# Attention block with group norm: the output projection in plain fp32 column halves instead of split fp32r weights

## The chip, the core and the metric

The kernel runs on one core of a Trainium2 chip. The metric is device time in microseconds of one execution, input in HBM to output in HBM. Before the change it is 1597.04 us, the median of three runs (1596.77 to 1597.25).

## What is computed

```python
# x: (4, 512, 48, 48) fp32; t = 48 * 48 = 2304 tokens; 8 heads of d = 64; C = 512
hn  = group_norm(x)                         # 32 groups of 16 channels, with scale and bias
qkv = einsum('oc,bchw->bohw', qkv_w, hn) + qkv_b
q, k, v = fp16 parts of qkv.reshape(b, 3, 8, 64, t)
w   = softmax(einsum('bhct,bhcs->bhts', q * s, k * s))   # s = 64 ** -0.25 in fp16
a   = einsum('bhts,bhcs->bhct', w, v).astype(float32)
out = x + einsum('oc,bchw->bohw', proj_w, a) + proj_b
```

## The kernel before

**Tiling.** Channels lie on the 128 partitions, in NC = 4 chunks c. The 2304 tokens of a batch are cut into NQ = 5 blocks j, four of 512 columns and one of 256. Heads go in pairs: 4 pairs a batch, 16 pairs g in all, one head in partitions 0 to 63 and one in 64 to 127.

**The main stream.** The attention is a list of steps, `stream`, each of them three score tiles: six score matmuls (`scores`, L1066) and three exponentials on ScalarE (L1073), two steps later the weighted values into the bank `av` (`values`, L1091), and on VectorE the running sum of the exponentials (`add`, L1122). At a block's end a ones matmul gives the softmax sums (`sl`, L1150); VectorE copies them (`rows`, `slx`), two DMAs gather them in the tile `sums`, GpSimd tests whether they lie between two bounds (`check_sums`, L1188 and L1189), VectorE inverts them, DMAs spread the inverses over the partitions (`ib`), and GpSimd divides into the fp16 tile `att` (`divide`, L1215). The tests accumulate in `fine`; if one fails, a flag selects a general path at the very end.

**Side work.** Chains of matmuls for q and k (`pqk`, L802), v (`pv`, L854) and the output projection (`pr`, L948) stand in a list, `beside`. `fill(n)` issues from it at each step, after the weighted values and ahead of the next scores (in a step that closes a block, ahead of the weighted values), by nominal costs that are written in the code, 1.77 us for a projection chain of 512 columns. All side chains share one PSUM bank, `pw`. Nothing is reordered after that: each engine runs its instructions in the order of issue.

**The projection.** `att32` copies att in fp32 into tiles `a` (ScalarE or GpSimd, L942 and L940). The matmul form fp32r reads those as fp32 in reduced precision, so the weights are split ahead of time into a high part `whi` and a low part `wlo`, the remainder. For each row block m, `proj_chain` adds up four c, each with whi and wlo, 128 weight columns wide: 8 matmuls. VectorE adds the bias and the residual x that was loaded two chains earlier into one of RES = 4 tiles (`residual`, tag `res`; L975), and SyncE's queue stores the tile. Batch 0 is projected while batch 1 is attended, and so on. In the last batch blocks 2 to 4 are projected in two parts: three pairs c (FIRST) while the last pair is attended, the fourth (LAST) after it. The last nine steps stand in the tail, in the banks `ahead`, `rest`, `held` and `last_av`.

The qkv weights and the normalized x are plain fp32, and the q, k and v chains are written in two column halves, `lo` in (0, 64), each into its half of the bank's partitions.

The functions that the change touches, and what calls them:

Of the kernel before, what the change touches and what calls it, by code (L numbers as in the profile page):

```python
# [470 lines left out]
def fast_path(  # L471
# [11 lines left out]
):  # L483
    nc = tc.nc

    RES = NC
    const = ctx.enter_context(tc.tile_pool(name="const", bufs=1))
    xpool = ctx.enter_context(tc.tile_pool(name="xpool", bufs=1))
    qkp = ctx.enter_context(tc.tile_pool(name="qkp", bufs=3))
# [11 lines left out]
    hn = {}  # L501


    SPARE = {(1, 2): lambda c: ("res", RES), (1, 3): lambda c: (f"a32_{c}", 1)}

    def load_x(b, j, c, engine):

# [46 lines left out]
    nc.sync.dma_start(bv, brow.to_broadcast((P, C)))  # L554


    whi = const.tile([P, NC, C], F32R, name="whi")
    wlo = const.tile([P, NC, C], F32R, name="wlo")

    wproj = {}  # L560

    def load_wproj(c):
        wproj[c] = work.tile([P, C], F32, tag="res", bufs=RES, name=f"wproj_{c}")
        nc.sync.dma_start(wproj[c], proj_wT[bass.ts(c, P), :])

    def split_wproj(c):
        w = wproj.pop(c)
        nc.vector.tensor_copy(whi[:, c, :], w)
        nc.vector.tensor_tensor(
            wlo[:, c, :], w, whi[:, c, :].bitcast(F32), ALU.subtract  # L570
        )

    mhalf = const.tile([P, 2], F32, name="mhalf")
    nc.gpsimd.memset(mhalf, -0.5)
# [15 lines left out]
            channel_multiplier=sign,  # L590
        )

    fine = const.tile([P, 2 * QB // P], F32, name="fine")
    nc.gpsimd.memset(fine, 1.0)

# [310 lines left out]
    def in_two(b, j):  # L908

        return b == B - 1 and j >= NQ - 3  # L910
# [13 lines left out]
    def att32(b, j, pairs=range(NC), beside=None):  # L924
        o, n = QBLOCKS[j]
        for c in pairs:
            if left_over(b, j):
                t = xpool.tile([P, n], F32R, tag=f"x{c}_{j}", name=f"a32_{b}_{j}_{c}")
            elif in_two(b, j) and c in EARLY:
                t = xpool.tile(  # L930
                    [P, n], F32R, tag=f"x{2 * c + 1}_1", name=f"a32_{b}_{j}_{c}"
                )
            else:
                t = work.tile(
                    [P, QB], F32R, tag=f"a32_{c}", bufs=1, name=f"a32_{b}_{j}_{c}"
                )
            at32[b, j, c] = t[:, :n]
            source = atts[b * NPAIR + c][:, o : o + n]
            if beside or c in beside_exps() and not (pairs == LAST and left_over(b, j)):
                nc.gpsimd.tensor_copy(at32[b, j, c], source)  # L940
            else:
                nc.scalar.copy(at32[b, j, c], source)  # L942

    def proj_chain(b, j, m, ps, pairs=range(NC)):
        n = QBLOCKS[j][1]
        steps = [(c, w) for c in pairs for w in (whi, wlo)]
        for i, (c, w) in enumerate(steps):
            nc.tensor.matmul(  # L948
                ps[:, :n],
                w[:, c, bass.ts(m, P)],  # L950
                at32[b, j, c],
                start=(i == 0),
                stop=(i == len(steps) - 1),
            )

    FIRST, LAST = range(NC - 1), range(NC - 1, NC)

# [26 lines left out]
    def proj_piece(b, j, chunks, pairs=range(NC), ahead=None):  # L984
        def run():
            evacuate, store = proj_run(b, j, chunks, pairs)
            evacuate()
            if pairs == LAST:
                finished.add((j, chunks[0]))

            if pairs != FIRST:
                loads.append((now[0] + 1, store))
            if ahead is not None:
                loads.append((now[0] + 1, ahead))

        return piece(QB / 290.0 * len(pairs) / NC, run, True, True)

    def proj_pieces(b, j):

        def ahead(k):
            if k < len(proj_list) and not in_two(b, proj_list[k][0]):
                residual(b, *proj_list[k])

        def begin():
            if in_two(b, j):
                att32(b, j, LAST)
            elif (b, j) == (B - 1, 0):
                att32(b, j, range(len(EARLY), NC))  # L1010
            else:
                att32(b, j)
            if j == 0:
                ahead(0)
                ahead(1)

        pairs = LAST if in_two(b, j) else range(NC)
        chains = [
            proj_piece(b, j, chunks, pairs, lambda k=k: ahead(k + 2))
            for k, (jj, chunks) in enumerate(proj_list)  # L1020
            if jj == j
        ]
        return [piece(0.0, begin)], chains
# [138 lines left out]
    def rows(g, j, sl):  # L1162

        o, n = QBLOCKS[j]
        sx = work.tile([P, QB], F32, tag="rows", name=f"slx_{g}_{j}")
        nc.vector.tensor_copy(sx[:, :n], sl[:, :n])  # L1166
        sm = small.tile([P, 2, QB // P], F32, tag="sums", name=f"sums_{g}_{j}")
        for h in range(2):
            nc.sync.dma_start(sm[:, h, : n // P], sx[h * D : h * D + 1, :n])
        sums[g, j] = sm  # L1170
        return sx
# [7 lines left out]
        )  # L1179

    def check_sums(g, j):
        n = QBLOCKS[j][1]
        sm = sums[g, j][:, :, : n // P]
        ok = fine.rearrange("p (h i) -> p h i", h=2)[:, :, : n // P]
        for op, limit in ((ALU.is_ge, SUM_MIN), (ALU.is_le, SUM_MAX)):
            t = small.tile([P, 2, QB // P], F32, tag="in", name=f"in_{g}_{j}")
            t = t[:, :, : n // P]
            nc.gpsimd.tensor_scalar(t, sm, limit, None, op)  # L1188
            nc.gpsimd.tensor_tensor(ok, ok, t, ALU.mult)  # L1189

    def invert(g, j):
        n = QBLOCKS[j][1]
# [124 lines left out]
    for b in range(B):  # L1317
        g = b * NPAIR
        old = b - 1
        if b == 0:  # L1320
            for j in range(NQ):
                if j < NC:
                    put_run(load_wproj, j)
                if j > 0:
                    put_run(split_wproj, j - 1)
                put_qk(g + 1, 1, (j,))
                put_qk(g + 1, 0, (j,))
            for block in SPARE:
                put_run(reload, *block)
        put_qk(g + 2, 1)  # L1330
        put_qk(g + 2, 0)

        late = [j for j in range(NQ) if (b + 1, j) in SPARE]
        early = [j for j in range(NQ) if j not in late]
        tiles = {j: range(o // P, (o + n) // P, 2) for j, (o, n) in enumerate(QBLOCKS)}
        for j in early:
            put_v(b, 1, tiles[j])
        if b == B - 1:
            put_qk(g + 3, 1)
            put_qk(g + 3, 0, range(NQ - 1))  # L1340
            put_convert(old, 0)
            put_qk(g + 3, 0, (NQ - 1,))

            THIRD = range(len(EARLY), NC - 1)
            ahead = [
                (residual, b, j, chunks)
                for j in (NQ - 2, NQ - 3, NQ - 1)
                for jj, chunks in proj_list
                if jj == j
            ]  # L1350
            ahead += [
                (att32, b, j, (c,)) for j in (NQ - 2, NQ - 3, NQ - 1) for c in EARLY
            ]
            ahead.append((att32, b, NQ - 2, THIRD))
            for j in range(NQ):
                put_proj(old, j, ahead)
                if j + 1 < NQ:
                    put_convert(old, j + 1)
            assert not ahead

            ahead = [
                (att32, b, NQ - 3, THIRD),
                (att32, b, NQ - 1, THIRD),
                *((att32, b, 0, (c,), True) for c in EARLY),
            ]
            for j in (NQ - 2, NQ - 3, NQ - 1):
                put_first(b, j, ahead if j != NQ - 2 else [])
            put_convert(b, 0)
            put_proj(b, 0)
            put_convert(b, 1)  # L1370
            put_proj(b, 1)
            put_convert(b, NQ - 3)
            put_proj(b, NQ - 3)
            continue

        for j in early:
            if j == NQ - 1 and b > 0:
                put_convert(old, 0)
            put_qk(g + 3, 1, (j,))
            put_qk(g + 3, 0, (j,))  # L1380
            put_run(reload, b + 1, j)
        for j in late:
            put_v(b, 1, tiles[j])
            put_qk(g + 3, 1, (j,))
            put_qk(g + 3, 0, (j,))
        if b > 0:
            for j in range(NQ - 1):
                put_proj(old, j)
                put_convert(old, j + 1)
        put_v(b + 1, 0)  # L1390
        if b > 0:
            put_proj(old, NQ - 1)
        put_qk(g + 4, 1)
        put_qk(g + 4, 0)
        put_qk(g + 5, 1)
        put_qk(g + 5, 0)
# [116 lines left out]
    for n in range(end):  # L1513
# [20 lines left out]
        if n >= BEHIND and not inside:  # L1534
            values(stream[n - BEHIND])
        if block_at(n - BEHIND - 2):
            check_sums(*block_at(n - BEHIND - 2))
            invert(*block_at(n - BEHIND - 2))
        if block_at(n - BEHIND - 3):
            spread(*block_at(n - BEHIND - 3))  # L1540
# [2 lines left out]
            divide(*block_at(n - BEHIND - 4))  # L1543
        if not filled:
            fill(n)
        while joins:
            joins.popleft()()
        if n - BEHIND in soon:
# [153 lines left out]
```

## Time and profile before

| | |
|---|---|
| runs | 1596.77, 1597.04, 1597.25 us |
| profiled execution | span 1595.6 us, first to last instruction (1.4 us under the median; a time of its own is not listed beside the span) |
| TensorE clock granted | 0.999 of full |
| projection, L948 | 640 matmul records, 155.4 us busy |
| q and k, L802 | 2560 matmul records, 536.2 us busy |
| GpSimd's range test, L1188 and L1189 | 158 instructions each, 100.8 and 62.0 us |
| HBM | 60.7 MB read, 19.2 MB written, 50 GB/s over the span |

Each engine runs its own queue in order: PE (TensorE matmuls), PEld (its weight loads, beside the matmuls), DVE (VectorE), ACT (ScalarE), POOL (GpSimd), SP (SyncE, DMA issue). A row of groups reads: line, engine, operation, out<-in, shapes, count, then busy us and mean ns of one, then the idle time ahead of them and what ended it. In rows of PE, 128*64 is weight rows times weight columns. A busy time counts modelled ends of matmuls, which reach into the next; the distance from start to start is free of that. In a timeline row like instructions are merged (x16), and its first number is the start of the first.

### The profile page before, as it was taken

To read this page: it belongs to the slowest core of one execution; us is meant where nothing else is said; L and a number is where in the kernel's file an instruction comes from. 1 tells how busy PE (TensorE), PEld (TensorE's weight loads), DVE (VectorE), ACT (ScalarE), POOL (GpSimd) and SP (SyncE) were. 2 spreads that over 40 slices of the span, in tenths; PEclk is the share of its full clock that TensorE was granted. 3 is DMA by queue.
4 is the path that set the end of the run, shared out by engine and by line. 5 is a ranking of instruction groups with operands and counts; after the bars stand their busy time and mean duration, and the time that the engine had idled before them with its cause. 6 is when DMAs were issued, how large, how long until landed. Compare 5 with 4: busy or idle time off the path is not lost. (4 is left out here: it accounts for less than half of the span.)

```text
span 1595.6 us, 28731 instructions
## 1 busy us (share of the span) xinstructions
PE 1582.0 (99%) x11526; PEld 701.7 (44%) x11526; DVE 1140.2 (71%) x1302; ACT 1269.4 (80%) x1363; POOL 336.8 (21%) x463
## 2 busy tenths in 40 slices
PE   9999999999999999999999999999999999999997
PEld 3733434443333534545333354455533334434554
DVE  6267668876666678887666666888767676767776
ACT  4177777888888888888888888887878888888885
POOL 1001202222121222312112121222212121121232
PEclk9999999999999999999999999999999999999999
DMA  7002020000000024521000001353101000015424
GB/s 222 3 14 67 12 73 16 18 14 12 15 18 11 12 69 119 144 67 28 11 14 18 14 12 41 111 158 88 23 17 18 15 15 11 15 31 166 149 62 133
DMA packets 94896, 82.10 MB, mean 51 GB/s; under 512 B 50852, under 2 KB 60964, under 8 KB 94756
## 3 DMA queue, kind: packets, MB, share of 16 engines
q1 hardware_dynamic: 92724, 78.35, 18.1%
q8 instruction: 92, 1.51, 0.4%
q10 hardware_dynamic: 1904, 1.84, 0.4%
q14 instruction: 48, 0.39, 0.1%
q0 software_dynamic: 128, 0.01, 0.0%
HBM read 60.70 MB, written 19.17 MB: 50 GB/s over the span
## 5 line engine op out<-in xcount | busy, mean ns | idle before, releaser
L1073 ACT ACTIVATE p<-ps 128x1024 f16<-128x1024 f32 x1296 | 1233.5, 1025 | 299.1 <-PE ps L1066 296.3
L1122 DVE TENSOR_TENSOR acc<-acc,p 128x3072 f16<-128x3072 f16 x270 | 485.4, 1798 | 53.8 <-ACT p L1073 51.3
L802 PE MATMUL pqk<-x,wqkv 128*64 128x512 f32 (+1 forms) x2432 | 510.3, 549 | 0.1
L1091 PE MATMUL av<-p,v 128*64 128x512 f16 (+1 forms) x2880 | 360.6, 364 | 0.0
L1066 PE MATMUL ps<-q,k 64*128 64x512 f16 (+1 forms) x2880 | 355.8, 358 | 0.4 <-DVE v L862 0.2
L854 PE MATMUL pv<-wqkv,x 128*64 128x256 f32 x2304 | 267.6, 379 | 0.3 <-DVE v L862 0.3
L802 PEld LDWEIGHTS pqk<-x,wqkv 128*64 128x64 f32 x2432 | 168.5, 137 | 205.4 <-issue 155.9
L1188 POOL TENSOR_SCALAR in<-sums 128x8 f32<-128x8 f32 (+1 forms) x158 | 100.8, 638 | 712.4 <-DMA sums<-slx 705.8
L1066 PEld LDWEIGHTS <-k 64*128 64x128 f16 x2880 | 105.9, 94 | 287.2 <-issue 238.2
L1091 PEld LDWEIGHTS <-v 128*64 128x64 f16 x2880 | 131.2, 109 | 212.8 <-issue 168.1
L1215 POOL TENSOR_TENSOR att<-avx,ib 128x512 f16<-128x512 f32 (+1 forms) x78 | 133.1, 1706 | 422.9 <-DMA ib<-row 373.7
L854 PEld LDWEIGHTS pv<-wqkv,x 128*64 128x64 f32 x2304 | 166.3, 137 | 81.3 <-DVE v L862 0.8
L1122 DVE TENSOR_TENSOR acc<-p,p 128x3072 f16<-128x3072 f16 x79 | 138.1, 1748 | 0.0
L948 PE MATMUL pr<-a,whi 128*128 128x512 f32 (+1 forms) x311 | 121.8, 399 | 0.1
L1127 DVE TENSOR_TENSOR acc<-acc 128x1024 f16<-128x1024 f16 x156 | 114.7, 735 | 3.3
L948 PE MATMUL pr<-a,wlo 128*128 128x512 f32 (+1 forms) x311 | 113.5, 372 | 0.0
L813 DVE TENSOR_SCALAR q<-pqk,bqkv 128x512 f16<-128x512 f32 (+1 forms) x77 | 53.5, 694 | 76.0 <-PE pqk L802 75.5
L813 DVE TENSOR_SCALAR k<-pqk,bqkv 128x512 f16<-128x512 f32 (+1 forms) x75 | 52.2, 695 | 77.7 <-PE pqk L802 77.5
L862 DVE TENSOR_TENSOR v<-pv,bv 128x512 f16<-128x512 f32 x72 | 49.7, 690 | 79.6 <-PE pv L854 79.5
L1166 DVE COPY slx<-sl 128x512 f32<-128x512 f32 (+1 forms) x79 | 50.6, 641 | 64.1 <-PE sl L1150 64.1
L975 DVE SCALAR_TENSOR_TENSOR r<-pr,bproj,r 128x512 f32<-128x512 f32 (+1 forms) x80 | 54.9, 695 | 41.3 <-PE pr L948 36.6
L1100 DVE COPY avx<-av 128x512 f32<-128x512 f32 (+1 forms) x79 | 50.6, 640 | 36.4 <-PE av L1091 36.1
(124 smaller groups left out, 506.7 us busy)
## 6 DMA issues: line engine op xcount, KB each, us to landing
r<-x_dram SPq DMA_DIRECT2D x72, 256.0 KB, 3.6
out_dram<-r SPq DMA_DIRECT2D x69, 256.0 KB, 2.4
ib<-row SPq DMA_DIRECT2D x126, 128.0 KB, 3.1
x<-x_dram SPq DMA_DIRECT2D x62, 256.0 KB, 3.9
x<-x_dram SPq DMA_DIRECT2D x16, 128.0 KB, 4.8
sums<-slx SPq DMA_DIRECT2D x128, 2.0 KB, 2.1
ib<-row SPq DMA_DIRECT2D x30, 64.0 KB, 3.0
wqkv<-qkv_wT_dram SPq DMA_DIRECT2D x2, 768.0 KB, 6.9
```

The costliest lines, as they stand in the source:

```text
L802: nc.tensor.matmul(pw[0][lo : lo + D, :n], wqkv[:, c, w0 + lo : w0 + lo + D], hn[b, c, j], start=(c == 0), stop=(c == NC - 1),)
L813: nc.vector.tensor_scalar(qk[g][part][:, o : o + n], pw[0][:, :n], bqkv[:, col : col + 1], SCALE, ALU.add, ALU.mult,)
L854: nc.tensor.matmul(pw[0][lo : lo + D, a, :], hn[b, c, i * P // QB][:, at + lo : at + lo + D], wqkv[:, c, 2 * C + half * C // 2 :][:, : C / ...
L948: nc.tensor.matmul(ps[:, :n], w[:, c, bass.ts(m, P)], at32[b, j, c], start=(i == 0), stop=(i == len(steps) - 1),)
L975: nc.vector.scalar_tensor_tensor(xt[:, i], places[i], bias, xt[:, i], ALU.add, ALU.add)
L1066: nc.tensor.matmul(ps[:, h, a * n : (a + 1) * n], kt[rows, bass.ts(i, P)], qt[rows, o : o + n], start=True, stop=True,)
L1073: nc.scalar.activation(pt[:, r], ps, AF.Exp)
L1091: nc.tensor.matmul(av[0][lo : lo + D, :n], vv[b, pr // 2][:, i, pr % 2 * P + lo : pr % 2 * P + lo + D], pt[:, r, h, a * n : (a + 1) * n], ...
L1122: nc.vector.tensor_tensor(t, before, pt, ALU.add)
L1127: nc.vector.tensor_tensor(t[:, 0], t[:, 0], t[:, r], ALU.add)
L1188: nc.gpsimd.tensor_scalar(t, sm, limit, None, op)
L1215: nc.gpsimd.tensor_tensor(atts[g][:, o : o + n], avx.pop((g, j))[:, :n], ibs.pop((g, j))[:, :n], ALU.mult,)
```

## The change

The projection's weights stay in plain fp32 in one tile `wproj`; `whi`, `wlo` and the eight VectorE instructions of the split are gone. `proj_chain` takes, for each c, the two column halves lo = 0 and 64 in place of whi and wlo, with `a` in fp32. There are six residual tiles instead of four, and residuals are loaded four chains ahead instead of two; the tiles `a` for chunks 2 and 3 get a second copy. The sums go into two standing tiles `sums_0` and `sums_1` that pairs use in turn, and `check_sums` tests a pair's 40 columns at once after its last block (for the last pair in two parts), issued behind the division and the filler instead of ahead of them.

```diff
-    RES = NC
+    RES = NC + 2
+    LEAD = RES - 2
+    def copies(c):
+        return 1 if c < NC // 2 else 2
...
-    whi = const.tile([P, NC, C], F32R, name="whi")
-    wlo = const.tile([P, NC, C], F32R, name="wlo")
+    wproj = const.tile([P, NC, C], F32, name="wproj")
...
-        nc.sync.dma_start(wproj[c], proj_wT[bass.ts(c, P), :])
-
-    def split_wproj(c):
-        w = wproj.pop(c)
-        nc.vector.tensor_copy(whi[:, c, :], w)
-        nc.vector.tensor_tensor(
-            wlo[:, c, :], w, whi[:, c, :].bitcast(F32), ALU.subtract
-        )
+        nc.sync.dma_start(wproj[:, c, :], proj_wT[bass.ts(c, P), :])
...
+    for s in range(2):
+        t = const.tile([P, NQ, 2, QB // P], F32, name=f"sums_{s}")
+        nc.gpsimd.memset(t, SUM_MIN)
+        sums_of.append(t)
...
                 t = work.tile(
-                    [P, QB], F32R, tag=f"a32_{c}", bufs=1, name=f"a32_{b}_{j}_{c}"
+                    [P, QB], F32, tag=f"a32_{c}", bufs=copies(c), name=f"a32_{b}_{j}_{c}"
                 )
...
     def proj_chain(b, j, m, ps, pairs=range(NC)):
         n = QBLOCKS[j][1]
-        steps = [(c, w) for c in pairs for w in (whi, wlo)]
-        for i, (c, w) in enumerate(steps):
-            nc.tensor.matmul(
-                ps[:, :n],
-                w[:, c, bass.ts(m, P)],
-                at32[b, j, c],
-                start=(i == 0),
-                stop=(i == len(steps) - 1),
-            )
+        for c in pairs:
+            for lo in (0, D):
+                nc.tensor.matmul(
+                    ps[lo : lo + D, :n],
+                    wproj[:, c, m * P + lo : m * P + lo + D],
+                    at32[b, j, c],
+                    start=(c == pairs[0]),
+                    stop=(c == pairs[-1]),
+                )
...
             if j == 0:
-                ahead(0)
-                ahead(1)
+                for k in range(LEAD):
+                    ahead(k)
...
-            proj_piece(b, j, chunks, pairs, lambda k=k: ahead(k + 2))
+            proj_piece(b, j, chunks, pairs, lambda k=k: ahead(k + LEAD))
...
-        sm = small.tile([P, 2, QB // P], F32, tag="sums", name=f"sums_{g}_{j}")
+        sm = sums_of[g % 2][:, j]
...
+        ends = (NQ - 1,) if g < NG - 1 else (NQ - 3, NQ - 2)
+        if j not in ends:
+            return
+        first = NQ - 2 if g == NG - 1 and j == NQ - 2 else 0
+        cols = slice(first * PER, (j + 1) * PER)
...
         if block_at(n - BEHIND - 2):
-            check_sums(*block_at(n - BEHIND - 2))
             invert(*block_at(n - BEHIND - 2))
...
         if not filled:
             fill(n)
+        if block_at(n - BEHIND - 2):
+            check_sums(*block_at(n - BEHIND - 2))
```

On PE, the first projection chain of batch 0, with the score weight load that follows it. Before (`pr` is the bank, `a` the copies of att):

```order
L948 MATMUL pr_0_0_6427<-a_0_0_0_6292,whi 128x512
L948 MATMUL pr_0_0_6427<-a_0_0_0_6292,wlo 128x512
L948 MATMUL pr_0_0_6427<-a_0_0_1_6294,whi 128x512
L948 MATMUL pr_0_0_6427<-a_0_0_1_6294,wlo 128x512
L948 MATMUL pr_0_0_6427<-a_0_0_2_6296,whi 128x512
L948 MATMUL pr_0_0_6427<-a_0_0_2_6296,wlo 128x512
L948 MATMUL pr_0_0_6427<-a_0_0_3_6298,whi 128x512
L948 MATMUL pr_0_0_6427<-a_0_0_3_6298,wlo 128x512
L1066 LDWEIGHTS k_4172
```

The same place on PE after the change, with the last matmul ahead of it; x2 stands for two rows that read alike, the two column halves:

```order
L1093 MATMUL av_3_6181<-p_3_2_6140,v_1_2956 64x512
L948 MATMUL pr_0_0_6256<-a_0_0_0_6124,wproj 64x512 x2
L948 MATMUL pr_0_0_6256<-a_0_0_1_6126,wproj 64x512 x2
L948 MATMUL pr_0_0_6256<-a_0_0_2_6128,wproj 64x512 x2
L948 MATMUL pr_0_0_6256<-a_0_0_3_6130,wproj 64x512 x2
L1068 LDWEIGHTS k_4069
```

The chain keeps its place and its eight matmuls; each now covers 64 output rows instead of 128. Elsewhere on PE almost nothing moves.

On PE at the end of the program, the last six steps, before:

```order
L948 MATMUL rest_16551<-a_3_3_3_16473,whi 128x512
L948 MATMUL rest_16551<-a_3_3_3_16473,wlo 128x512
L948 MATMUL rest_16551<-a_3_3_3_16473,whi 128x512
L948 MATMUL rest_16551<-a_3_3_3_16473,wlo 128x512
L948 MATMUL held<-a_3_4_3_16560,whi 128x256
L948 MATMUL held<-a_3_4_3_16560,wlo 128x256
L948 MATMUL held<-a_3_4_3_16560,whi 128x256
L948 MATMUL held<-a_3_4_3_16560,wlo 128x256
L948 MATMUL last_av<-a_3_4_3_16560,whi 128x256
L948 MATMUL last_av<-a_3_4_3_16560,wlo 128x256
L948 MATMUL last_av<-a_3_4_3_16560,whi 128x256
L948 MATMUL last_av<-a_3_4_3_16560,wlo 128x256
```

And after, from `ahead` to the matmul that counts the tests:

```order
L948 MATMUL ahead_16075<-a_3_2_3_15869,wproj 64x512 x2
L948 MATMUL rest_16086<-a_3_3_3_16013,wproj 64x512 x4
L948 MATMUL rest_16091<-a_3_3_3_16013,wproj 64x512 x4
L948 MATMUL held<-a_3_4_3_16100,wproj 64x256 x4
L948 MATMUL last_av<-a_3_4_3_16100,wproj 64x256 x4
L1646 MATMUL count<-ones,good 1x1
```

The number of matmuls and their order are the same here too.

On GpSimd, the first blocks of pair 0, before (`in` and `fine` are the range test, `att` the division, NO_OP a placeholder):

```order
L1188 TENSOR_SCALAR in_0_1019<-sums_0_975 128x8
L1189 TENSOR_TENSOR fine<-fine,in_0_1019 128x8
L1188 TENSOR_SCALAR in_0_1022<-sums_0_975 128x8
L1189 TENSOR_TENSOR fine<-fine,in_0_1022 128x8
L780 NO_OP x2
L1215 TENSOR_TENSOR att_748<-avx_0_943,ib_0_1065 128x512
```

And after, from block 3 of the same pair on:

```order
L1220 TENSOR_TENSOR att_750<-avx_3_1652,ib_3_1781 128x512
L780 NO_OP
L1193 TENSOR_SCALAR in_4_1883<-sums_167 128x40
L1194 TENSOR_TENSOR fine<-fine,in_4_1883 128x40
L1193 TENSOR_SCALAR in_4_1886<-sums_167 128x40
L1194 TENSOR_TENSOR fine<-fine,in_4_1886 128x40
L780 NO_OP x2
L1220 TENSOR_TENSOR att_750<-avx_4_1779,ib_4_1911 128x256
```

The divisions of blocks 0 to 3 have no test ahead of them any more, and one test of 40 columns stands where the last block's was.

More of the change, by code (lines that the diff above doesn't have):

```diff
@@ L501, in fast_path @@
     hn = {}
-    SPARE = {(1, 2): lambda c: ("res", RES), (1, 3): lambda c: (f"a32_{c}", 1)}
+    SPARE = {(1, 2): lambda c: ("res", RES), (1, 3): lambda c: (f"a32_{c}", copies(c))}
     def load_x(b, j, c, engine):
@@ L554, in fast_path @@
     nc.sync.dma_start(bv, brow.to_broadcast((P, C)))
-    whi = const.tile([P, NC, C], F32R, name="whi")
-    wlo = const.tile([P, NC, C], F32R, name="wlo")
-    wproj = {}
+    wproj = const.tile([P, NC, C], F32, name="wproj")
     def load_wproj(c):
-        wproj[c] = work.tile([P, C], F32, tag="res", bufs=RES, name=f"wproj_{c}")
-        nc.sync.dma_start(wproj[c], proj_wT[bass.ts(c, P), :])
-    def split_wproj(c):
-        w = wproj.pop(c)
-        nc.vector.tensor_copy(whi[:, c, :], w)
-        nc.vector.tensor_tensor(
-            wlo[:, c, :], w, whi[:, c, :].bitcast(F32), ALU.subtract
-        )
+        nc.sync.dma_start(wproj[:, c, :], proj_wT[bass.ts(c, P), :])
     mhalf = const.tile([P, 2], F32, name="mhalf")
@@ L591, in fast_path @@
         )
-    fine = const.tile([P, 2 * QB // P], F32, name="fine")
+    PER = 2 * QB // P
+    fine = const.tile([P, NQ * PER], F32, name="fine")
     nc.gpsimd.memset(fine, 1.0)
+    sums_of = []
+    for s in range(2):
+        t = const.tile([P, NQ, 2, QB // P], F32, name=f"sums_{s}")
+        nc.gpsimd.memset(t, SUM_MIN)
+        sums_of.append(t)
     alone = [True]
@@ L927, in att32 @@
             if left_over(b, j):
-                t = xpool.tile([P, n], F32R, tag=f"x{c}_{j}", name=f"a32_{b}_{j}_{c}")
+                t = xpool.tile([P, n], F32, tag=f"x{c}_{j}", name=f"a32_{b}_{j}_{c}")
             elif in_two(b, j) and c in EARLY:
                 t = xpool.tile(
-                    [P, n], F32R, tag=f"x{2 * c + 1}_1", name=f"a32_{b}_{j}_{c}"
+                    [P, n], F32, tag=f"x{2 * c + 1}_1", name=f"a32_{b}_{j}_{c}"
                 )
@@ L1002, in ahead @@
         def ahead(k):
-            if k < len(proj_list) and not in_two(b, proj_list[k][0]):
+            if k >= len(proj_list) or in_two(b, proj_list[k][0]):
+                return
+            if (b, proj_list[k][0], proj_list[k][1][0]) not in res:
                 residual(b, *proj_list[k])
@@ L1181, in check_sums @@
     def check_sums(g, j):
-        n = QBLOCKS[j][1]
-        sm = sums[g, j][:, :, : n // P]
-        ok = fine.rearrange("p (h i) -> p h i", h=2)[:, :, : n // P]
+        ends = (NQ - 1,) if g < NG - 1 else (NQ - 3, NQ - 2)
+        if j not in ends:
+            return
+        first = NQ - 2 if g == NG - 1 and j == NQ - 2 else 0
+        cols = slice(first * PER, (j + 1) * PER)
+        sm = sums_of[g % 2].rearrange("p j h i -> p (j h i)")[:, cols]
         for op, limit in ((ALU.is_ge, SUM_MIN), (ALU.is_le, SUM_MAX)):
-            t = small.tile([P, 2, QB // P], F32, tag="in", name=f"in_{g}_{j}")
-            t = t[:, :, : n // P]
+            t = small.tile([P, NQ * PER], F32, tag="in", name=f"in_{g}_{j}")[:, cols]
             nc.gpsimd.tensor_scalar(t, sm, limit, None, op)
-            nc.gpsimd.tensor_tensor(ok, ok, t, ALU.mult)
+            nc.gpsimd.tensor_tensor(fine[:, cols], fine[:, cols], t, ALU.mult)
     def invert(g, j):
@@ L1323, in fast_path @@
                     put_run(load_wproj, j)
-                if j > 0:
-                    put_run(split_wproj, j - 1)
                 put_qk(g + 1, 1, (j,))
@@ L1364, in fast_path @@
                 *((att32, b, 0, (c,), True) for c in EARLY),
+                *((residual, b, *proj_list[k]) for k in range(2)),
             ]
```

## The prediction

> **What bounds the kernel now.** I read the page's busy shares first, then the stretches in which projections run, then single chains on TensorE's timeline.
>
> ```profile
> PE 1582.0 (99%) x11526; PEld 701.7 (44%) x11526; DVE 1140.2 (71%) x1302; ACT 1269.4 (80%) x1363; POOL 336.8 (21%) x463
> L1073 ACT ACTIVATE p<-ps 128x1024 f16<-128x1024 f32 x1296 | 1233.5, 1025 | 299.1 <-PE ps L1066 296.3
> ```
>
> A busy PE alone proves little, since ends of matmuls are modelled. The second row says it from the other side: ScalarE, next in load, stands idle 299.1 us ahead of its exponentials, and 296.3 us of that ends with a score matmul. The exponentials wait for PE, not PE for them. The stretches (start:end, length, then busy time and records by engine) show whether that holds where projections run; the second row has none.
>
> ```profile
> 629.00:749.00 120.00, 120.00 (x931) 66.70 (x930) 100.52 (x131) 99.53 (x110) 30.69 (x39) 1.00 0.32 90
> 749.00:1036.00 287.00, 287.00 (x2089) 112.24 (x2089) 200.81 (x208) 239.29 (x253) 58.83 (x82) 1.00 0.13 32
> 1440.00:1577.00 137.00, 136.85 (x868) 73.36 (x866) 101.27 (x109) 119.65 (x136) 39.43 (x53) 1.00 0.45 131
> ```
>
> In both projection stretches PE has no idle time worth naming (0 and 0.15 us), at a granted clock of 1.00; VectorE has 19.5 and 35.7 us left, ScalarE 20.5 and 17.3. So what a projection chain takes on PE, from its first matmul to the first matmul of the next work, is paid in full, and the case reduces to that price before and after.
>
> **The chain before.** A full chain is four steps c, each with whi and wlo, 128 weight columns wide. Timeline of PE, columns start and duration in us:
>
> ```profile
> 639.79 0.50 PE L948 MATMUL pr<-a,whi 128*128 128x512 f32 x1
> 640.13 0.39 PE L948 MATMUL pr<-a,wlo 128*128 128x512 f32 x1
> 640.36 0.40 PE L948 MATMUL pr<-a,whi 128*128 128x512 f32 x1
> ...
> 641.53 0.40 PE L948 MATMUL pr<-a,wlo 128*128 128x512 f32 x1
> 641.86 0.83 PE L1066 MATMUL ps<-q,k 64*128 64x256 f16 x12
> ```
>
> Inside the chain a record follows the last at 0.23 us (640.13 to 640.36): a split weight costs one record each for whi and wlo. The chain holds PE for 641.86 - 639.79 = 2.07 us.
>
> **The chain after.** Plain fp32 weights in two halves of 64 columns against an fp32 moving tile of 512: this form is in the trace already, as the q/k chains (L802) and, 256 wide, as the v chains (L854).
>
> ```profile
> L802 PE MATMUL pqk<-x,wqkv 128*64 128x512 f32 x1936 | 451.7, 592 | 0.1
> 373.40 3.60 PE L802 MATMUL pqk<-x,wqkv 128*64 128x512 f32 x16
> 376.83 0.81 PE L1091 MATMUL av<-p,v 128*64 128x512 f16 x6
> 808.24 3.60 PE L802 MATMUL pqk<-x,wqkv 128*64 128x512 f32 x16
> 811.77 0.82 PE L1066 MATMUL ps<-q,k 64*128 64x512 f16 x6
> 339.21 3.62 PE L854 MATMUL pv<-wqkv,x 128*64 128x256 f32 x32
> 342.77 0.82 PE L1066 MATMUL ps<-q,k 64*128 64x512 f16 x6
> ```
>
> A whole q/k chain is written as 4 steps of 2 halves, 8 matmuls; the trace has 16 records, two per matmul. It holds PE for 3.43 us where the weighted values follow and 3.53 us where scores follow: 0.86 us a step, plus 0.10 us for the turn to the 64-row score matmuls. Halves run beside each other, but each needs twice the records and each pair of records takes 0.43 us. So the new chain stands in the program with as many matmuls as the old one and holds PE 1.36 to 1.46 us longer.
>
> **The sum.** How many chains there are follows from the loops (4 batches x 4 row blocks m x 4 steps c, for four blocks j of 512 columns and one of 256: 256 and 64 steps), and the records by shape bear it out: 251 and 60 of whi below, and 5 and 4 under the tail's names.
>
> ```profile
> L948 PE MATMUL pr<-a,whi 128*128 128x512 f32 x251 | 106.4, 424 | 0.1
> L948 PE MATMUL pr<-a,whi 128*128 128x256 f32 x60 | 15.4, 295 | 0.0
> 1503.86 0.39 PE L948 MATMUL pr<-a,whi 128*128 128x256 f32 x1
> ...
> 1505.96 0.82 PE L1066 MATMUL ps<-q,k 64*128 64x512 f16 x6
> 1516.89 0.50 PE L948 MATMUL pr<-a,whi 128*128 128x512 f32 x1
> ...
> 1518.48 0.84 PE L1091 MATMUL av<-p,v 128*64 128x512 f16 x6
> 1577.61 0.50 PE L948 MATMUL pr<-a,whi 128*128 128x512 f32 x1
> ...
> 1578.27 1.50 PE L1091 MATMUL av<-p,v 128*64 128x256 f16 x24
> ```
>
> - Full chains of 512: 16 in each of three batches and 8 in the last, 56. If all stand before scores 56 x (3.53 - 2.07) = 81.8 us, if none does 56 x (3.43 - 2.07) = 76.2. A filler is issued after the weighted values and ahead of the next scores, except in steps that close a block, so I take 81.
> - Pieces of two 256 chains, 2 in each of three batches: from 2.10 us (1503.86 to 1505.96) to the v row's 3.56: 6 x 1.46 = 8.8.
> - Last batch, three steps c (FIRST), 8 of 512 columns: from 1.59 us (1516.89 to 1518.48) to 3 x 0.86 + 0.10 = 2.68: 8.7. The 2 pieces of 256, at six of eight steps of the same rows: 2 x (2.67 - 1.58) = 2.2.
> - Single steps (LAST) issued beside the last blocks: 3, from 0.66 us (1577.61 to 1578.27) to 0.86 to 0.96: 0.9.
>
> That is 101.6 us up to the tail. The tail has nine more steps, and there PE isn't alone on the path:
>
> ```profile
> 1582.33 0.50 PE L948 MATMUL ahead<-a,whi 128*128 128x512 f32 x1
> 1583.10 0.59 ACT L1592 COPY beyond_ahead<-ahead 128x512 f32<-128x512 f32 x1
> 1583.15 0.50 PE L948 MATMUL rest<-a,whi 128*128 128x512 f32 x1
> 1584.12 1.29 POOL L1595 TENSOR_TENSOR r<-beyond_ahead,r 128x512 f32<-128x512 f32 x1 [0.46 <-ACT beyond_ahead L1592]
> 1586.08 0.28 PE L948 MATMUL last_av<-a,wlo 128*128 128x256 f32 x1
> 1588.13 0.43 DVE L1640 TENSOR_REDUCE good<-fines 128x1 f32<-128x264 f32 x1 [0.49 <-POOL fines L1627]
> 1588.48 0.68 DVE L971 TENSOR_TENSOR r<-last_av,r 128x512 f32<-128x512 f32 x1
> ```
>
> Now the last output's addition starts at 1588.48, 2.1 us after PE is through with it, because VectorE does `good` first, which waits for GpSimd. After: `ahead` ends at 1582.33 + 0.86 = 1583.19, four `rest` steps at 1586.6, four steps of 256 columns at 0.43 at 1588.3 and their data some 0.25 later. The copy of `ahead` moves 0.4 later and GpSimd's row of work behind it too, so `good` starts near 1588.5 and the addition near 1588.9. PE's 2.2 us are nearly covered; +0.4 remains.
>
> 101.6 + 0.4 = 102.0 us on the profiled execution's span of 1595.6, which lies 1.4 below the median of the runs, 1597.04. Forecast: 1699 us, 6.4% slower.
>
> **The parts that cost nothing.** Covers and bounds, by rows:
>
> ```profile
> L1188 POOL TENSOR_SCALAR in<-sums 128x8 f32<-128x8 f32 (+1 forms) x158 | 100.8, 638 | 712.4 <-DMA sums<-slx 705.8
> L568 DVE CAST whi<-wproj 128x512 fp32r<-128x512 f32 x4 | 1.7, 417 | 0.0
> L569 DVE TENSOR_TENSOR wlo<-wproj,whi 128x512 fp32r<-128x512 f32 x4 | 2.8, 693 | 0.1
> PEld pr L948 <- DVE r L975: 4.9, 15, 0.6
> ```
>
> The split goes: 4.5 us of VectorE in batch 0, where PE runs the q/k chains of L802, idle 0.1 us in all ahead of them. The range test goes from 158 pairs of GpSimd instructions to 34 on up to 40 columns and moves behind the division; GpSimd is busy 21% and was waiting for the sums' DMAs anyway, so the division starts a little sooner, which no chain needs. The sums' DMAs now write one of two standing tiles in turn, last read one pair's length earlier, about 1596 / 16 = 100 us, so no queue stalls on it. The four weight loads and 72 residual loads are the same in number; residual loads go two chains earlier on SyncE's queue into two more tiles, well ahead of their use. Copies of att write fp32 in place of fp32r; the trace shows none of that kind, and I take the old duration, with ScalarE's 17 us and more of slack in each stretch as cover. What could be gained from more tiles is bounded by waits around the chains: weight loads waited 4.9 us for the addition that frees the bank, but beside a PE that was still streaming. I take 0, with -5 as the far end.
>
> **Rivals.**
> - *Half the records.* If a plain fp32 half needed one record instead of two, a step would take 0.43 us and a full chain 4 x 0.43 + 0.10 = 1.82, shorter than 2.07: 56 x -0.25, with the shorter ones in proportion another -4, gives -18, 1579 us. It decides from a step below 0.49 us. For it speaks that both programs have eight matmuls per chain; against it 16 records in each whole q/k chain. The Trainium skill, "Perfetto Trace Analysis", section "Engine Utilization", has TensorE's output rate merely halved for FP32_LOW_HIGH, which is this rival; "FP8 and Floating Point Precision", section "TensorE Precision Notes", has true fp32 as four passes. By the first the step is 0.43 us, by the second 0.85, both as estimates; the measured 0.86 sides with the second. Chance 0.02.
> - *PE isn't the limit there.* If exponentials set the pace in the projection stretches, a chain's extra time would vanish in PE's waits: 1597. Against it stand the full PE and ScalarE's 20 us of idle time in 120. Chance 0.01.
> - *Waits go too.* The added tiles and lighter VectorE and GpSimd take the 4.9 us out after all: 1694. Chance 0.05.
> - *A longer end.* The tail pays PE's full 2.2 us, or as much again where 640 more matmul records shift what each engine has fetched by then, which no row prices; 4 us in all, an estimate: 1703. Chance 0.05.
>
> **How the numbers follow.** The main case has 0.87. Its terms vary between the two follower prices (-5 us if all stand before weighted values, +1 if all before scores) and the tail's 0 to +2. Low end 1692, where the waits go too and part of the follower term; high end 1705, a longer end with all chains at the dearer price and a microsecond of spread. A change of 0.2%, 3.2 us, is what can be told from none. Faster 0.02 (half the records), same 0.01 (PE not the limit), slower 0.97.
>
> **What would show it.** Right: L948 has twice the matmul records, 64 columns wide; a full chain takes 3.4 to 3.5 us; the three projection stretches grow by about 26, 26 and 49 us (16 x 1.45 + 2 x 1.46 for one batch, the rest of the sum for the last), PE still full and ScalarE idle longer; the rest of the program keeps its length. Wrong: chains near 1.8 us, or PE with idle time beside projections, or another stretch that changes by more than 3 us.

## The result

The changed kernel takes 1691.78 us, median of five runs (1691.31 to 1692.12), beside 1597.04 before: 94.7 us more, ratio 1.0594 (95% interval 1.0581 to 1.0607). The forecast was 1699, range 1692 to 1705. It is too high by 7.2 us, and the measured time lies just below the range.

The page after: busy shares, the chain that ended last (by engine), ScalarE's exponentials, the projection.

```profile
PE 1678.5 (99%) x12166; PEld 686.5 (41%) x12166; DVE 1136.1 (67%) x1294; ACT 1270.3 (75%) x1363; POOL 218.6 (13%) x217
PE 98%; DVE 1%; DMA 0%; ACT 0%; issue 0%; POOL 0%; DVEq 0%
L1075 ACT ACTIVATE p<-ps 128x1024 f16<-128x1024 f32 x1296 | 1233.3, 1025 | 391.8 <-PE ps L1068 390.4
L948 PE MATMUL pr<-a,wproj 128*64 128x512 f32 (+1 forms) x1244 | 254.1, 552 | 0.0
```

640 more matmul records, all of the projection. The exponentials take as long as before (1233.3 beside 1233.5) and wait 94.1 us more for PE (390.4 beside 296.3): PE's added time reaches the end one for one. GpSimd's busy time fell by 118.2 us (218.6 beside 336.8) and VectorE's by 4.1, and neither shows in the time. The stretches with projections (start:end, length, busy by engine) still have a full PE:

```profile
629.00:773.00 144.00, 144.00 (x1088) 62.41 (x1086) 99.89 (x131) 99.73 (x110) 17.56 (x19) 1.00 0.25 74
1060.00:1205.00 145.00, 144.84 (x1056) 60.80 (x1052) 101.21 (x128) 100.34 (x111) 21.81 (x19) 1.00 0.26 73
1490.00:1671.00 181.00, 181.00 (x1166) 66.03 (x1166) 99.63 (x109) 118.89 (x135) 32.46 (x33) 1.00 0.32 96
```

From the first projection record of one batch to that of the next (629.0, 1035.6 and 1445.5 us before, 628.9, 1060.0 and 1494.2 after) the program grew by 24.5 and 24.4 us, and from the last of these to the end by 45.6; ahead of the first it kept its length. The forecast had 26, 26 and 49. Each of the three stretches came out shorter than forecast, so the missing 7 us are not in one place; spread over some 75 chains they are about a tenth of a microsecond each.

**Where they are.** Here is one chain after, in PE's timeline, with the work ahead of it and behind it, and then, of the kernel before, weighted values ahead of a projection chain and ahead of a q/k chain:

```profile
658.31 0.85 PE L1093 MATMUL av<-p,v 128*64 128x256 f16 x12
658.99 3.60 PE L948 MATMUL pr<-a,wproj 128*64 128x512 f32 x16
662.52 0.82 PE L1068 MATMUL ps<-q,k 64*128 64x512 f16 x6
```

```profile
639.02 0.84 PE L1091 MATMUL av<-p,v 128*64 128x512 f16 x6
639.79 0.50 PE L948 MATMUL pr<-a,whi 128*128 128x512 f32 x1
...
407.70 0.84 PE L1091 MATMUL av<-p,v 128*64 128x512 f16 x6
408.38 1.88 PE L802 MATMUL pqk<-x,wqkv 128*64 128x512 f32 x8
```

The chain after holds PE for 662.52 - 658.99 = 3.53 us, the forecast price. But look at the weighted values *ahead* of a chain, before: six matmuls hold PE for 0.77 us where a projection follows (639.02 to 639.79) and for 0.68 where a q/k chain follows. From the last of them to the next matmul pass 0.31 us in the one case and 0.21 in the other (medians over 56 and 180 places). The projection's old chain was 128 weight columns wide and its neighbours are 64: the turn into it cost 0.10 us, and that time stands in front of the chain's first record, under another line. It isn't the weight load's wait for the bank: at 42 of the 56 places the profile shows no engine or transfer that the chain's first weight load waited for, and the gap there is 0.309 or 0.310 us; where VectorE's addition was waited for, it is 0.309 or 0.310 in five of seven, 0.329 and 0.526 in the others. After the change the weighted values ahead of a projection end at 0.21 us like all others. Over the whole trace, from start to start, the projection's own records went from 152.6 to 254.5 us (+101.8, forecast 102.0), the weighted values from 303.7 to 297.2 us (-6.5) and the sums' matmuls (`sl`) from 23.4 to 22.4 (-1.0): together +94.4 from the unrounded sums, beside 94.3 by the spans (1689.9 and 1595.6).

### The profile page after: what moved, and what is told of

It is laid out like the page before. It is cut to its first block, busy times and chain, and to the rows that moved or that the text cites. A ratio compares the mean times of both kernels' runs of the same rounds, so it can differ in the third digit from the quotient of the medians.

```text
span 1689.9 us, 29737 instructions
## 1 busy us (share of the span) xinstructions
PE 1678.5 (99%) x12166; PEld 686.5 (41%) x12166; DVE 1136.1 (67%) x1294; ACT 1270.3 (75%) x1363; POOL 218.6 (13%) x217
## 4 chain that ended last, share of the span: by engine, by line
PE 98%; DVE 1%; DMA 0%; ACT 0%; issue 0%; POOL 0%; DVEq 0%
PE pqk L802 28%; PE ps L1068 19%; PE av L1093 19%; PE pv L854 15%; PE pr L948 14%; PE sl L1152 2%; PE ps L802 1%; DMA x<-x_dram 0%; PE rest L948 0%; PE first_w L802 0%; PE first_av L802 0%; DVE st L624 0%; DVE r L971 0%; ACT p L1075 0%; DVE v L862 0%
## 5 line engine op out<-in xcount | busy, mean ns | idle before, releaser
L1075 ACT ACTIVATE p<-ps 128x1024 f16<-128x1024 f32 x1296 | 1233.3, 1025 | 391.8 <-PE ps L1068 390.4
L1220 POOL TENSOR_TENSOR att<-avx,ib 128x512 f16<-128x512 f32 (+1 forms) x78 | 123.7, 1586 | 1347.8 <-DMA ib<-row 1141.9
L948 PE MATMUL pr<-a,wproj 128*64 128x512 f32 (+1 forms) x1244 | 254.1, 552 | 0.0
L948 PEld LDWEIGHTS pr<-a,wproj 128*64 128x64 f32 x1244 | 86.8, 137 | 125.0 <-issue 105.2
L1129 DVE TENSOR_TENSOR acc<-acc 128x1024 f16<-128x1024 f16 x156 | 111.1, 712 | 3.3
L624 DVE BATCH_NORM_STATS2 st<-x 128x6 f32<-128x512 f32 (+1 forms) x80 | 47.0, 625 | 3.0 <-DMA x<-x_dram 3.0
```

The source lines that it names most:

```text
L948: nc.tensor.matmul(ps[lo : lo + D, :n], wproj[:, c, m * P + lo : m * P + lo + D], at32[b, j, c], start=(c == pairs[0]), stop=(c == pairs[-1]),
L1075: nc.scalar.activation(pt[:, r], ps, AF.Exp)
L1129: nc.vector.tensor_tensor(t[:, 0], t[:, 0], t[:, r], ALU.add)
L1220: nc.gpsimd.tensor_tensor(atts[g][:, o : o + n], avx.pop((g, j))[:, :n], ibs.pop((g, j))[:, :n], ALU.mult,)
```

## The experiments

**The projection's form alone.** The kernel before, with old tiles and old range test; the tiles `a` become plain fp32 and the split goes as well. The lines that matter:

```diff
-    whi = const.tile([P, NC, C], F32R, name="whi")
-    wlo = const.tile([P, NC, C], F32R, name="wlo")
+    wproj = const.tile([P, NC, C], F32, name="wproj")
...
-        steps = [(c, w) for c in pairs for w in (whi, wlo)]
...
+        for c in pairs:
+            for lo in (0, D):
+                nc.tensor.matmul(
+                    ps[lo : lo + D, :n],
+                    wproj[:, c, m * P + lo : m * P + lo + D],
+                    at32[b, j, c],
+                    start=(c == pairs[0]),
+                    stop=(c == pairs[-1]),
+                )
```

> The kernel before with the plain fp32 halves alone: old tiles, old range test per block. If the projection's form is the whole change, 1691.8 us like the changed kernel, within 1.5. Rival: the added tiles or the rarer range test took the 7 us that the forecast has too much; then this one takes 1697 to 1699.

1691.19 us (1691.01 to 1691.65), ratio 1.0588 (1.0574 to 1.0603). The form gives the whole change as far as can be told (0.6 us less than with the other edits), and the rival falls: added tiles and rarer tests didn't take the 7 us. The gap behind the weighted values is 0.21 us here as well.

**The range test alone.** The kernel before with `sums_0` and `sums_1`, and the test once per pair behind the division:

```diff
-            check_sums(*block_at(n - BEHIND - 2))
             invert(*block_at(n - BEHIND - 2))
...
         if not filled:
             fill(n)
+        if block_at(n - BEHIND - 2):
+            check_sums(*block_at(n - BEHIND - 2))
```

> The kernel before with the range test once per pair alone, behind the division. If it is off the path: 1597.0 us within 1.5. Rival: it is worth some of the 7 us, 1590 to 1595.

1596.51 us beside 1597.41 for the kernel before in the same comparison, ratio 0.9994 (0.9985 to 1.0003): no difference that can be told.

**Whole width instead of halves.** This takes the halves away from the changed kernel and leaves fp32:

```diff
-            for lo in (0, D):
-                nc.tensor.matmul(
-                    ps[lo : lo + D, :n],
-                    wproj[:, c, m * P + lo : m * P + lo + D],
+            nc.tensor.matmul(
+                ps[:, :n],
+                wproj[:, c, bass.ts(m, P)],
```

> The changed kernel with one edit: plain fp32 weights 128 columns wide in place of two halves. Theory A (the turn into a chain is paid when the weights' width changes from 64 to 128 columns, at the last gap of the work ahead, 0.10 us a chain in the trace of before): the last weighted-value matmul ahead of a chain is followed at 0.31 us again, not 0.21, and with 0.02 us more a record, as fp32r's 128-column records show, a full chain takes about 3.75 us: 1716 us, +24 on the changed kernel. Theory B (the turn belongs to the fp32r form): the gap stays at 0.21, and the time is 1692 to 1709.

1708.01 us, ratio 1.0694 (1.0678 to 1.0711); +16.7 on the changed kernel by the spans (1706.6 and 1689.9). Its PE timeline:

```profile
701.65 0.84 PE L1092 MATMUL av<-p,v 128*64 128x512 f16 x6
702.42 3.70 PE L947 MATMUL pr<-a,wproj 128*128 128x512 f32 x8
706.06 0.82 PE L1067 MATMUL ps<-q,k 64*128 64x512 f16 x6
```

The weighted values take 0.77 us again, with a last gap of 0.31 us: that is theory A on the gap, with a format that isn't fp32r. The time falls into theory B's span all the same, since A was priced too high: the records have no 0.02 us more each (0.429 us from start to start, as in halves), only the first one 0.10. So fp32r's 0.23 us a record, where 512 columns take 0.21 in fp16, is that form's own. A whole chain takes 3.63 us against 3.53 in halves. Two records a step one after the other, or four in pairs side by side: halves don't make plain fp32 cheaper, a step is 0.86 us either way.

**Two fp16 parts in place of two fp32r parts.** att is fp16 already, so fp16 weights can meet it without fp32 copies. From the kernel before, in column halves:

```diff
-    whi = const.tile([P, NC, C], F32R, name="whi")
-    wlo = const.tile([P, NC, C], F32R, name="wlo")
+    whi = const.tile([P, NC, C], F16, name="whi")
+    wlo = const.tile([P, NC, C], F16, name="wlo")
...
-    apool = ctx.enter_context(tc.tile_pool(name="apool", bufs=2 * NPAIR - 1))
+    apool = ctx.enter_context(tc.tile_pool(name="apool", bufs=2 * NPAIR))
...
     def att32(b, j, pairs=range(NC), beside=None):
         for c in pairs:
+            at32[b, j, c] = atts[b * NPAIR + c][:, o : o + n]
...
         for i, (c, w) in enumerate(steps):
+            for lo in (0, D):
```

> The kernel before with weights split into two fp16 parts in place of two fp32r parts, in column halves, against the fp16 att itself (no fp32 copies, one more att tile). Each half pair should take 0.213 us as the weighted values do, a full chain 8 x 0.213 + 0.10 = 1.81 us, and the gap ahead of it 0.21: 56 x (1.81 - 2.17) = -20, the shorter chains -6, the tail -1: 1570 us. If halves of a chain don't run side by side, 16 x 0.21 = 3.4 us a chain and about 1685.

1584.99 us (1581.35 to 1587.18), ratio 0.9916 (0.9900 to 0.9931): 15 us more than expected. The chains are as expected, 1.83 us ahead of scores and 1.73 ahead of weighted values, entered at a median gap of 0.21. But the mean of that gap is 0.43 and its longest 2.44, and the waits (engine, line, whom for; us in total, times, longest) name a cause that the kernel before didn't have:

```profile
DVE r L961 <- DMA r<-x_dram: 11.2, 7, 2.6
PE pr L934 <- DVE r L961: 9.3, 9, 2.1
```

With shorter chains the residual tiles turn over faster than their loads arrive. VectorE waits for a residual and so holds the one bank `pw`, and PE waits for VectorE. The longest of these waits, and behind it a stretch of 4 us by engine:

```profile
1043.67 0.75 DVE L961 SCALAR_TENSOR_TENSOR r<-pr,bproj,r 128x512 f32<-128x512 f32 x1 [2.58 <-DMA r<-x_dram]
1044.47 0.41 PE L934 MATMUL pr<-att,whi 128*64 128x512 f16 x2 [2.06 <-DVE r L961]
1045.05 0.69 PE L934 MATMUL pr<-att,whi 128*64 128x512 f16 x2
1044.00:1048.00 4.00, 3.53 (x18) 1.60 (x19) 2.90 (x6) 0.10 (x1) 0.00 (x0) 0.59 0.46 138
```

The number behind the engines is the granted clock: 0.59 in these 4 us, 1.00 in the 14.5 us ahead of them. The chain behind the wait took 3.33 us instead of 1.83, so this wait cost another 1.5 us. Behind the next longest gap, 1.96 us, the chain took 1.85: one place, then, and no rule. The gaps' surplus, 56 x 0.22 = 12 us, and this make up most of what is missing in this run. It is the slowest of the four, which lie 5.8 us apart; the others have no profile. The rival of halves that don't run side by side (1685 us) falls.

**The same in whole width.** The kernel of the last experiment without the loop over `lo`, the old 128-column matmuls with fp16 parts:

> The kernel with two fp16 weight parts, but 128 columns wide in place of halves. If the turns belong to the width, not to fp32r: the gap from the last weighted-value matmul to the chain is 0.31 us at least, not 0.21, a chain of 8 records takes 8 x 0.21 + 0.2 = 1.9 us, and its stay on PE is 0.2 us longer than in halves on both ends together; 75 chains x 0.2 = +15 on the kernel in halves, less what of its waits this takes up: 1588 to 1600 us. If the turns belong to fp32r: gap 0.21, chain 1.8, 1585.

1582.29 us, ratio 0.9907 (0.9890 to 0.9923), less than the expected 1588 to 1600. The turn is there: a median gap of 0.312 us ahead of a chain, in fp16 as in fp32r and fp32. The chain takes 1.83 us, not 1.9, because the turn out of it, into the 64-row scores, is paid by halves too, and here the first record costs only 0.01 more. So width costs 0.1 us a chain here too, and still the kernel isn't slower than in halves: in its profiled run the wait for residual loads is gone, and PE's wait for VectorE is 0.6 us. Chains that are longer by the turns may just leave the loads time enough; that is not shown, and the runs of the two kernels overlap (1581.35 to 1587.18 in halves, 1581.97 to 1584.12 here). The first record's extra 0.10 us in fp32 and fp32r goes with longer weight loads:

```profile
L947 PEld LDWEIGHTS pr<-a,wproj 128*128 128x128 f32 x622 | 112.0, 189 | 118.4 <-issue 105.7 <-DVE acc L1128 3.7 <-ACT p L1074 3.6
L933 PEld LDWEIGHTS <-whi 128*128 128x128 f16 x320 | 31.1, 97 | 50.5 <-issue 27.1 <-DVE r L960 0.4
```

The first row is plain fp32 in whole width, the second fp16: 0.189 and 0.097 us for 128 columns. The gap ahead of the chain is 0.31 us in both, so that one isn't the weight load's length. Whether the load alone makes the first record's 0.10 wasn't tried apart.

**fp16 halves with the change's own tiles.** The changed kernel, with its six residual tiles, loads four chains ahead and the rare range test, and the fp16 parts in halves:

```diff
-    wproj = const.tile([P, NC, C], F32, name="wproj")
+    whi = const.tile([P, NC, C], F16, name="whi")
+    wlo = const.tile([P, NC, C], F16, name="wlo")
...
-                    wproj[:, c, m * P + lo : m * P + lo + D],
+                    w[:, c, m * P + lo : m * P + lo + D],
```

> The changed kernel (six residual tiles, loads four chains ahead, range test once per pair) with the fp16 weight parts in halves, no fp32 copies. In the kernel with the old four tiles the chains were 1.73 to 1.83 us as expected, but VectorE waited 11.2 us for residual loads and the gap ahead of a chain averaged 0.43 us, not 0.21: 56 x 0.22 = 12 us. If the two tiles more take these waits away: 1573 us. Rival: the loads are late because the queue or the stores are, and it stays at 1582 to 1587.

1575.62 us (1575.39 to 1576.62), ratio 0.9863 (0.9847 to 0.9880): the fastest here. The wait for residual loads is gone from the list and PE's for VectorE is down from 9.3 to 0.6:

```profile
PE pr L945 <- DVE r L972: 0.6, 2, 0.4
```

The same edits were worth nothing around fp32 chains (1691.78 with them, 1691.19 without) and are worth 9.4 us by the medians here, and at least 4.7 between any two of the runs. The run can't say which of them does it; the waits that went point to the residual tiles and their earlier loads. Beside whole width in fp16, where PE hardly waits either, the span is 6.5 us shorter (1573.7 and 1580.2), and from start to start the weighted values and the sums give 5.7 of it: the turns again, though these two kernels differ in the tiles and the range test as well. The mean gap ahead of a chain is still 0.26 us, not 0.21, which is most of the 2.6 us that are left to the expected 1573.

## Why the prediction was wrong, point by point

- *PE bounds the projection stretches.* Right. PE stayed full, and ScalarE's waits grew by 94.1 us, what the time grew by.
- *The price of the new chain.* Right to a hundredth for whole chains: 3.53 us ahead of scores and 3.43 ahead of weighted values, 3.55 for two chains of 256, 2.67 for three steps; 0.91 to 0.96 for one, where 0.86 to 0.96 was forecast. Plain fp32 takes two records a half, and the rival with half the records is out: 0.86 us a step is four times the 0.21 that 512 columns take in fp16. Of the two pages of the Trainium skill that were weighed, this bears out "FP8 and Floating Point Precision", section "TensorE Precision Notes", with four passes for true fp32.
- *The price of the old chain.* This step failed. It was read "from its first matmul to the first matmul of the next work", 2.07 us, and that was said to be paid in full. That window has the turn out of the chain and not the turn into it, which PE spends before the first record and the trace books on the work ahead. The full price was 2.17. In the sum, the terms 56 x (3.53 - 2.07) and its smaller companions were each 0.10 a chain too large, over 73 places where the work ahead was 64 columns wide: 7.3 us too much, beside the 7.5 by which the weighted values and sums shrank. The new chain has no such term, being as wide as its neighbours. The range had no room for it either: its low end allowed for the work that follows a chain and for waits, not for the work ahead.
- The row that shows it was within reach: the weighted values ahead of the first quoted chain run from 639.02 to 639.79. A median over the whole group doesn't show it, since 56 of 384 runs of weighted values don't move a median. The Trainium skill, "TensorEngine Tiling (Array Packing)", section "Key Properties", says that changing the tiling mode drains TensorE, without a figure. The traces show a cost at such a change, 0.10 us a turn in three number formats; that it is a drain no run here shows.
- *The tail.* Forecast +0.4, measured 6.29 to 6.91 us from `ahead` to the counting matmul, +0.6. The cover was as described, a little thinner: `good` starts at 1682.36, and the last addition 0.37 behind it.

```profile
1676.05 1.03 PE L948 MATMUL ahead<-a,wproj 128*64 128x512 f32 x4
1682.36 0.45 DVE L1645 TENSOR_REDUCE good<-fines 128x1 f32<-128x296 f32 x1
1682.96 0.19 PE L1646 MATMUL count<-ones,good 128*1 128x1 f32 x2 [0.72 <-DVE good L1645]
```

- *The parts that cost nothing.* Right, by the experiments on the form and the range test. The copies of att into plain fp32 take the old time too: ScalarE's 587 ns in the mean beside 588; GpSimd's mean rose from 729 to 943 ns, with a median of 0.61 us for 512 columns in both.
- *Waits go too* (1694) came nearest in time, for a reason that isn't so: the weight loads' wait for VectorE is gone from the list after, but the gap ahead of a chain was the same with and without it in all but two places. *A longer end* didn't come: from the counting matmul to the end of the span it is 6.9 us, as before it was 7.0.

## What to carry to other kernels

Price a stretch of matmuls from the last matmul of the work ahead to the first of the work behind, not from its own first record: a turn of the array between weight shapes is booked on whoever came before. Group the work ahead by what follows it; a median over all of it hides the turn. Edits around a chain (here more residual tiles, earlier loads and a rarer test, together) that are worth nothing while the chains are slow can be worth several microseconds once they are short, so an edit found useless is tried again after the next one.

## What the runs showed of the hardware

A turn between weight tiles of 128 x 64, 64 x 128 and 128 x 128 costs PE 0.10 us, ahead of the first record of the new shape, in fp16, fp32r and fp32 alike. From the last record of 512 columns to the next matmul pass, without a turn and with one: 0.213 to 0.216 and 0.306 to 0.312 us in fp16, 0.232 and 0.327 to 0.329 in fp32r, 0.43 and 0.52 in fp32. With 256 columns in fp16 it is 0.106 and 0.199 to 0.205, so the turn costs the same there. In one place a wait cost more than its own length: behind PE's 2.06 us of idle time, in the fp16 halves with four residual tiles, the granted clock was 0.59 over 4 us and a chain of 1.83 us took 3.33.

Plain fp32 costs 0.86 us for 128 x 128 weights and 512 columns, whole or in halves. fp32r costs 0.23 a record for 128 columns where fp16 costs 0.216, so two fp16 parts against an operand that is fp16 already are cheaper than two fp32r parts by 0.24 us in a chain of eight (2.07 and 1.83), before any other gain.
